# A selective scan in a two-layer block: the product with C on GpSimd, the scan's input in PSUM, channels in two halves

## The chip, the core and the metric

The kernel runs on one core of one Trainium2 chip. The core has five engines that work from queues of their own: TensorE (PE; PEld is its loading of weights), VectorE (DVE), ScalarE (ACT), GpSimd (POOL) and SyncE (SP), which here only starts DMAs. SBUF and PSUM are its on-chip memories of 128 partitions; matmuls write to PSUM, in 8 banks of 512 float32 columns. The metric is device microseconds of one execution, the median of several runs.

## The reference, cut to what matters

Two layers, each with adaptive normalisation, over 2048 tokens of width 512. The first is a block-masked linear layer and a gated feed-forward layer with low-rank additions. The second is a selective state-space layer (1024 channels, 16 states each) and a linear layer with a top-2 choice of low-rank experts. The change touches the second layer's scan, and the normalisations of both:

```python
def _layernorm(x, axis=-1, eps=1e-05):
    m = jnp.mean(x, axis=axis, keepdims=True)
    v = jnp.var(x, axis=axis, keepdims=True)
    return (x - m) / jnp.sqrt(v + eps)
...
dt = jax.nn.softplus(ts @ W_dt.T + b_dt)
A = -jnp.exp(A_log.astype(jnp.float32))

def step(state, inp):
    dt_t, B_t, C_t, u_t = inp
    dA = jnp.exp(dt_t[..., None] * A)
    state = state * dA + (dt_t * u_t)[..., None] * B_t[:, None, :]
    y = jnp.einsum('bdn,bn->bd', state, C_t)
    return (state, y)
...
y = ys.transpose(1, 0, 2) + x * D
y = y * jax.nn.silu(gate)
return y @ W_out.T
```

## The kernel before, in words

All is float32. The 2048 tokens are cut into 8 chunks of 256 (`TC`); a chunk's activations are two tiles of 128 tokens (`NM`) by 512. The 1024 channels of the scan are 8 tiles (`ND`) of 128 channels, one channel to a partition, with time along the columns.

For a chunk c and each of the 16 states n the loop at the end of the kernel does this:

- `decays` (L455): eight ScalarE exponentials, one per channel tile, write exp(dt * A) into `da` (two buffers, taken in turn).
- L669, VectorE: dt*u times row n of B, which is broadcast to all partitions, goes into `hb` (two buffers).
- L671, VectorE: one scan over 8 x 258 = 2064 columns, in place in `hb`. Each channel tile has two columns more than its 256 (`SEG = TC + 2`): one with zero decay that clears the state, and one that holds the state carried from the chunk before. `S.copy` at L681 puts it there from `states`, and L673 saves the new one.
- L677, VectorE: `hb` times row n of C goes into `hc` (two buffers).
- `add_t` (L438), TensorE: 16 transposes add `hc` to the accumulators `ys`, four PSUM banks with tokens on the partitions. They are issued one state later, behind the next scan (`due`).

`rows_bc` (L460) loads row n of B and C for a chunk by a broadcast DMA of 256 KB on SyncE's queue, three states ahead; four buffers. Behind the first state of a chunk, `gating` (L483) multiplies the finished `ys` of the chunk before by the gate, and `skip` (L446) begins the new sums with u*D. `steps` (L419: dt by a matmul and a softplus) and `inputs` (L429: dt*u) prepare the next chunk at its predecessor's last state.

The matmul work of the other layers is written as generators. The loop takes pieces of them at every state by a budget in microseconds of TensorE work: `first` runs the first layer of later chunks (`first_layer`, L265), `second` (`beside`, L622) the output projection (`out_proj`) of the chunk before, the gate projection (`gate_proj`), the front part of the next chunk (`front`: norm, input projection, convolution at L391) and the experts of the chunk before. Weights come from memory again for each chunk, in 256 KB loads on SyncE's queue, through 12 `ws` buffers. Within each engine's queue the instructions keep one fixed order, which the planner of the language chose.

`norm_t` (L144), four times per chunk, takes mean and variance on VectorE (L148, L149), the inverse root on GpSimd (L151, L152), applies both on VectorE (L156), and transposes on TensorE. In `front`, GpSimd also copies the convolution's three halo columns in and out (L379, L382). L256 is a GpSimd product of 128x512 in the preparation of weights, before the loop. PSUM is full: four banks for matmuls (`ps_mm`), four for `ys`.

Of the kernel before, what the change touches and what calls it, by code (L numbers as in the profile page):

```python
# [17 lines left out]
P = 128  # L18
# [5 lines left out]
R = 16  # L24
DI, NS, RDT, KC = 1024, 16, 32, 4
ND = DI // P
SEG = TC + 2
E = 8
EA = E * R
LN_EPS, RMS_EPS = 1e-5, 1e-6  # L30
# [7 lines left out]
def mamba_block_kernel(  # L38
# [17 lines left out]
    tpool = ctx.enter_context(tc.tile_pool(name="tmp", bufs=5))  # L56
    hpool = ctx.enter_context(tc.tile_pool(name="hT", bufs=1))
    hid = ctx.enter_context(tc.tile_pool(name="hid", bufs=6))
    upool = ctx.enter_context(tc.tile_pool(name="u", bufs=ND // 2))
    zpool = ctx.enter_context(tc.tile_pool(name="z", bufs=2 * NM))  # L60
    bcp = ctx.enter_context(tc.tile_pool(name="bc", bufs=4))
    dram = ctx.enter_context(tc.tile_pool(name="dram", bufs=1, space=DRAM))
    ps_mm = ctx.enter_context(tc.tile_pool(name="ps_mm", bufs=4, space=PSUM))
    ps_y = ctx.enter_context(tc.tile_pool(name="ps_y", bufs=1, space=PSUM))

    def tmp():
        return tpool.tile([P, DM], FP, tag="t", name="tmp")
# [7 lines left out]
    def halves(t):  # L75
        return t.rearrange("p (a n) -> p a n", a=2)
# [18 lines left out]
            nc.sync.dma_start(out=xt, in_=x_in[i * P : (i + 1) * P, :])  # L95
            xs[c].append(xt)

    da = [keep.tile([P, ND, SEG], FP, name=f"da{i}") for i in range(2)]
    hb = [keep.tile([P, ND, SEG], FP, name=f"hb{i}") for i in range(2)]
    hc = [keep.tile([P, ND, TC], FP, name=f"hc{i}") for i in range(2)]  # L100
    dtu = keep.tile([P, ND, TC], FP, name="dtu")
    dt = keep.tile([P, ND, TC], FP, name="dt")
    states = keep.tile([P, NS, ND], FP, name="states")

    def mod_weights(wmod, j, queue):
        wms = []
# [37 lines left out]
    def norm_t(xt, scale, shift, tag):  # L144
        st = small.tile([P, NM, 6], FP, tag="st", name="st")
        mv = small.tile([P, NM, 2], FP, tag="mv", name="mv")
        for m in range(NM):
            V.bn_stats(st[:, m, :], xt[m])  # L148
            V.bn_aggr(mv[:, m, :], st[:, m, :])  # L149
        rs = small.tile([P, NM], FP, tag="rs", name="rs")  # L150
        G.tensor_scalar(rs, mv[:, :, 1], LN_EPS, None, ALU.add)  # L151
        G.tensor_tensor(rs, rs, power, ALU.pow)  # L152
        xn = []
        for m in range(NM):
            t = tmp()
            V.tensor_scalar(t, xt[m], mv[:, m, 0:1], rs[:, m : m + 1], ALU.subtract, ALU.mult)  # L156
            xn.append(t)
        h = hpool.tile([P, NK, TC], FP, tag=tag, bufs=2 if tag == "h0" else 1, name="h")
        for k2 in range(NK // 2):
            ps = halves(bank())  # L160
            for i in range(2):
                k = 2 * k2 + i
                for m in range(NM):
                    T.transpose(ps[:, i, m * P : (m + 1) * P], xn[m][:, k * P : (k + 1) * P], ident)  # L164
            for i in range(2):
                k = 2 * k2 + i
                S.activation(  # L167
                    h[:, k, :], ps[:, i, :], AF.Identity, bias=shift[:, k : k + 1], scale=scale[:, k : k + 1]
                )
            yield 0.5  # L170
        return h
# [43 lines left out]
    sb, cb = (mod_col("a", c0_sb, wmod0, j, nc.scalar) for j in (3, 4))  # L215
    gb = mod_gate(scb0, wmod0, 5, nc.scalar)

    ranks = [hc[0].rearrange("p t n -> p (t n)")[:R, i * DM : (i + 1) * DM] for i in range(3)]
    wides = [t.rearrange("p t n -> p (t n)")[:R, :FF] for t in (da[0], da[1], hb[0])]
    for dst, src in zip(ranks + wides, (gate_a, up_a, down_bt, gate_bt, up_bt, down_a)):  # L220
        nc.gpsimd.dma_start(out=dst, in_=src)
    ga_r, ua_r, db_r = ranks
# [121 lines left out]
    S.activation(neg_a, ch[:, :, C_A : C_A + NS], AF.Exp)  # L344
    V.tensor_scalar(neg_a, neg_a, -1.0, None, ALU.mult)
    for t in da:
        G.memset(t[:, :, 0:2], 0.0)
    for t in hb:
        G.memset(t[:, :, 0:2], 0.0)
    G.memset(states, 0.0)  # L350

    halo = None
    fed = {}
# [62 lines left out]
        fed[c] = (h, us, ssm, bc)  # L416
        yield 0.5

    def steps(c):  # L419
        us, ssm = fed[c][1:3]  # L420
        for t in range(ND):
            ps = bank()
            T.matmul(
                ps[:, :TC], lhsT=wdt[:, t * P : (t + 1) * P], rhs=ssm[:RDT, :], start=True, stop=True
            )
            dst, src, b_dt = dt[:, t, :], ps[:, :TC], ch[:, t, C_DT : C_DT + 1]
            S.activation(dst, src, AF.Softplus, bias=b_dt)

    def inputs(c):  # L429
        us = fed[c][1]  # L430
        for t2 in range(ND // 2):
            V.tensor_tensor(
                dtu[:, 2 * t2 : 2 * t2 + 2, :], dt[:, 2 * t2 : 2 * t2 + 2, :], us[t2], ALU.mult
            )

    ys = [[ps_y.tile([P, DM], FP, name=f"y{m}{a}") for a in range(2)] for m in range(NM)]

    def add_t(t, src, first, last):  # L438
        for m in range(NM):
            a, i = t // 4, t % 4  # L440
            T.matmul(  # L441
                ys[m][a][:, i * P : (i + 1) * P], lhsT=src[:, m * P : (m + 1) * P], rhs=ident,
                start=first and i == 0, stop=last, is_transpose=True, skip_group_check=True,
            )

    def skip(c):  # L446
        us = fed[c][1]
        for t2 in range(ND // 2):
            ud = halves(tmp())
            for i in range(2):  # L450
                t = 2 * t2 + i
                S.activation(ud[:, i, :], us[t2][:, i, :], AF.Identity, scale=ch[:, t, C_D : C_D + 1])
                add_t(t, ud[:, i, :], True, False)

    def decays(n):  # L455
        d = da[n % 2]
        for t in range(ND):
            S.activation(d[:, t, 2:], dt[:, t, :], AF.Exp, scale=neg_a[:, t, n : n + 1])  # L458

    def rows_bc(c, n):  # L460
        bcn = bcp.tile([P, 2, TC], FP, tag="bcn", name="bcn")
        nc.sync.dma_start(out=bcn, in_=fed[c][3][:, n, :].partition_broadcast(P))
        return bcn

    zs = {}

# [13 lines left out]
            for m in range(NM):  # L480
                S.activation(zs[c][2 * m + a], acc[m], AF.Silu)  # L481

    def gating(c):  # L483
        for m in range(NM):
            for a in range(2):
                z = zs[c][2 * m + a]
                V.tensor_tensor(z, z, ys[m][a], ALU.mult)

    def out_proj(c):
        xt = xs[c]  # L490
# [131 lines left out]
    def beside(c):  # L622
# [9 lines left out]
        if c > 0:  # L632
            yield from experts(c - 1)

    for _ in front(0):
        pass
    steps(0)
    inputs(0)
    bcs = [rows_bc(0, n) for n in range(3)]
    decays(0)  # L640
    first = ahead()
    ended = False

# [7 lines left out]

    due = None
    left = 0.0
    for c in range(NC):
        second = beside(c)
        spare, finished = 0.0, False
        for n in range(NS):
            h, d, hcn, bcn = hb[n % 2], da[n % 2], hc[n % 2], bcs.pop(0)
            if n + 1 < NS:
                decays(n + 1)  # L660
            if n == NS - 3:
                while not finished:
                    cost = next(second, "end")
                    finished = cost == "end"
                    if cost is None:
                        run_first(0.1)
            if n == NS - 1 and c + 1 < NC:
                steps(c + 1)
            V.tensor_tensor(h[:, :, 2:], dtu, bcn[:, 0:1, :].to_broadcast([P, ND, TC]), ALU.mult)  # L669
            flat_h, flat_d = h.rearrange("p t n -> p (t n)"), d.rearrange("p t n -> p (t n)")  # L670
            V.tensor_tensor_scan(flat_h, flat_d, flat_h, 0.0, ALU.mult, ALU.add)  # L671
            if c + 1 < NC:
                S.copy(states[:, n, :], h[:, :, SEG - 1])  # L673
            if due is not None:
                for t in range(ND):
                    add_t(t, due[:, t, :], False, n == 0)
            V.tensor_tensor(hcn, h[:, :, 2:], bcn[:, 1:2, :].to_broadcast([P, ND, TC]), ALU.mult)  # L677
            due = hcn
            if n + 1 < NS or c + 1 < NC:
                if c + (n + 1) // NS > 0:  # L680
                    S.copy(hb[(n + 1) % 2][:, :, 1], states[:, (n + 1) % NS, :])  # L681
            if n == 0:
                if c > 0:
                    gating(c - 1)
                skip(c)
            if n + 3 < NS:
                bcs.append(rows_bc(c, n + 3))
            elif c + 1 < NC:
                bcs.append(rows_bc(c + 1, n + 3 - NS))
            if n == NS - 1 and c + 1 < NC:  # L690
                inputs(c + 1)
                decays(0)
            budget = 4.8 if c > 0 or n > 7 else 2.5
            spare += budget
            while spare > 0 and not finished:
                cost = next(second, "end")
                finished = cost == "end"
                if cost is None or finished:
                    break
                spare -= cost  # L700
            left = run_first(left + (3.6 if c > 0 or n > 7 else 8.0) + (0.0 if finished else max(spare, 0.0)))
            spare = min(spare, 0.0)
    for t in range(ND):
        add_t(t, due[:, t, :], False, True)
    gating(NC - 1)
    for gen in (first, out_proj(NC - 1), experts(NC - 1)):
        for _ in gen:
            pass
# [73 lines left out]
```

## Time and profile before

| | us |
|---|---|
| median of 3 runs (lowest to highest) | 1860.17 (1859.12 to 1862.04) |
| the profiled execution | 1859.38 |
| its span, first to last instruction | 1857.6 |
| first scan (L671) starts | 246.9 |
| last product with C (L677) ends | 1808.7 |
| first scan of a chunk to the first of the next, chunks 0 to 6 | 221, 206, 209, 198, 198, 201, 184 |

Spans and starts are counted from the first instruction. A row of the table of groups names line, engine, operation, output from inputs, shapes and count; behind the bar stand the busy time and the mean duration in ns, behind the next one the idle time of the engine just before the group, and what ended it. L numbers are lines of the kernel before, and of the changed kernel where the text says so. In the waits, a line says which engine and line waited for which, how long in total, how often, and the longest. In the timeline, a line is a piece of one engine's work: start, length, line, operation.

### The profile page before, as it was taken

How to read it: one execution, taken by the hardware profiler on the slowest of the kernel's cores; microseconds unless marked ns; L12 is line 12 of the kernel's file. 1: busy time of each engine (PE TensorE's matmuls, PEld its weight loads, DVE VectorE, ACT ScalarE, POOL GpSimd, SP SyncE). 2: the span in 40 equal slices, each digit the busy share in tenths (PEclk: the TensorE clock that was granted, in tenths of full speed). 3: DMA queues.
4: the chain of work that ended last, by engine and by line, in shares of the span. 5: the costliest groups of instructions: out<-in, count | busy, mean ns of one | idle time of the engine just before them, and what ended most of it. 6: DMA issues, size and time to landing. Idle time of an engine off the chain costs nothing. (4 is left out here: it accounts for less than half of the span.)

```text
span 1857.6 us, 18733 instructions
## 1 busy us (share of the span) xinstructions
PE 1562.9 (84%) x6568; PEld 1079.8 (58%) x6568; DVE 1483.0 (80%) x1215; ACT 938.9 (51%) x2005; POOL 225.7 (12%) x211
## 2 busy tenths in 40 slices
PE   4899879988698888999799888999899789768646
PEld 4685647756465665576456665576557565544433
DVE  2222387797978989897999789897989799999992
ACT  0110367445654565565565566466556555674521
POOL 0123010013000200031003300160003000300000
PEclk9689779988998989999899999999999999879768
DMA  8544333562343234432343334422333235213100
GB/s 251 154 154 165 116 86 115 166 198 85 91 126 108 86 93 120 129 102 89 91 137 106 94 100 123 116 83 89 116 115 100 80 104 149 67 35 100 28 20 12
DMA packets 157536, 199.73 MB, mean 108 GB/s; under 512 B 14962, under 2 KB 93682, under 8 KB 157443
## 3 DMA queue, kind: packets, MB, share of 16 engines
q1 hardware_dynamic: 141984, 166.57, 31.0%
q10 hardware_dynamic: 10434, 15.81, 2.6%
q0 software_dynamic: 5024, 16.16, 2.4%
q8 instruction: 52, 0.85, 0.2%
q14 instruction: 42, 0.34, 0.1%
HBM read 182.43 MB, written 16.06 MB: 107 GB/s over the span
## 5 line engine op out<-in xcount | busy, mean ns | idle before, releaser
L671 DVE TENSOR_TENSOR_SCAN hb<-da,hb 128x2064 f32<-128x2064 f32 x128 | 568.7, 4449 | 3.5
L458 ACT ACTIVATE da<-dt,neg_a 128x256 f32<-128x256 f32 x1024 | 430.4, 497 | 55.9 <-DVE hb L671 43.1
L298 PE MATMUL ps<-h,ws 128*128 128x256 f32 (+1 forms) x1408 | 352.6, 407 | 19.6 <-ACT z L481 13.0
L441 PE MATMUL y<-ident,hc 128*128 128x128 f32 x2048 | 287.0, 293 | 65.5 <-DVE hc L677 65.3
L298 PEld LDWEIGHTS ps<-h,ws 128*128 128x128 f32 (+1 forms) x1408 | 281.6, 204 | 93.2 <-issue 19.6
L441 PEld LDWEIGHTS y<-ident,hc 128*128 128x128 f32 x2048 | 255.1, 152 | 117.8 <-DVE hc L677 75.4
L677 DVE TENSOR_TENSOR hc<-hb,bcn 128x2048 f32<-128x2048 f32 x128 | 291.4, 2278 | 35.8 <-PE y L441 35.6
L669 DVE TENSOR_TENSOR hb<-dtu,bcn 128x2048 f32<-128x2048 f32 x128 | 290.7, 2281 | 2.7
L673 ACT COPY states<-hb 128x8 f32<-128x8 f32 x112 | 22.8, 203 | 348.0 <-DVE hb L671 340.1
L151 POOL TENSOR_SCALAR rs<-mv 128x2 f32<-128x2 f32 x32 | 41.3, 1292 | 1155.4 <-DVE mv L149 1139.5
L508 PE MATMUL ps<-ws,tmp 128*128 128x512 f32 x256 | 136.3, 671 | 47.3 <-ACT tmp L502 47.1
L317 PE MATMUL ps<-ws,hidden 128*128 128x512 f32 (+1 forms) x352 | 159.0, 601 | 5.7 <-ACT z L481 4.9
L371 PE MATMUL ps<-h,ws 128*128 128x256 f32 x512 | 122.2, 394 | 2.5 <-ACT h L167 2.5
L476 PE MATMUL ps<-ws,h 128*128 128x512 f32 x256 | 117.1, 604 | 1.1 <-ACT hidden L306 0.6
L317 PEld LDWEIGHTS ps<-ws,hidden 128*128 128x128 f32 (+1 forms) x352 | 65.7, 192 | 85.1 <-issue 71.7
L371 PEld LDWEIGHTS ps<-h,ws 128*128 128x128 f32 x512 | 100.3, 199 | 21.3 <-ACT h L167 5.8
L508 PEld LDWEIGHTS ps<-ws,tmp 128*128 128x128 f32 x256 | 51.2, 214 | 101.3 <-ACT tmp L502 53.5
L309 DVE TENSOR_TENSOR hidden<-hidden,tmp 128x512 f32<-128x512 f32 x40 | 27.6, 690 | 85.1 <-ACT tmp L307 85.1
L391 DVE SCALAR_TENSOR_TENSOR tmp<-xp,ch,tmp 128x256 f32<-128x256 f32 x192 | 79.7, 476 | 13.1 <-ACT tmp L386 12.6
L458 ACT ACT_TABLE_LOAD x67 | 86.0, 1283 | 1.0
L164 PE MATMUL ps<-ident,tmp 128*128 128x128 f32 x256 | 48.7, 329 | 41.4 <-DVE tmp L156 38.0
L379 POOL COPY xp<-halo 128x6 f32<-128x6 f32 x28 | 71.0, 2537 | 77.2 <-DVE tmp L391 66.7
(137 smaller groups left out, 1575.0 us busy)
## 6 DMA issues: line engine op xcount, KB each, us to landing
bcn<-bc SPq DMA_DIRECT2D x128, 256.0 KB, 5.1
ws<-gate_s SPq DMA_DIRECT2D x70, 256.0 KB, 2.7
ws<-up_s SPq DMA_DIRECT2D x70, 256.0 KB, 2.7
ws<-down_s SPq DMA_DIRECT2D x70, 256.0 KB, 3.8
ws<-win_x_t_dram SPq DMA_DIRECT2D x64, 256.0 KB, 3.8
ws<-win_z_t_dram SPq DMA_DIRECT2D x64, 256.0 KB, 2.9
ws<-wout_s SPq DMA_DIRECT2D x64, 256.0 KB, 2.6
ws<-wmod_dram ACTq DMA_DIRECT2D x36, 256.0 KB, 3.2
```

The costliest lines, as they stand in the source:

```text
L298: T.matmul(ps[:n, i, :], lhsT=w3[:, k, :], rhs=h[:, k, :], stop=k == NK - 1, **start_only(4 * i + k),)
L317: T.matmul(acc[m], lhsT=hidden[j // 2][:n, j % 2, m * P : (m + 1) * P], rhs=w[:n, :], start=j == 0, stop=j == len(HT) - 1,)
L371: T.matmul(ps[:, i, :], lhsT=w3[:, k, :], rhs=h[:, k, :], stop=k == NK - 1, **start_only(4 * i + k),)
L379: G.tensor_copy(xp[:, :, : KC - 1], halo[:, 2 * t2 : 2 * t2 + 2, :])
L391: V.scalar_tensor_tensor(acc[:, i, :], xp[:, i, j : j + TC], ch[:, t, C_W + j : C_W + j + 1], acc[:, i, :], ALU.mult, ALU.add,)
L441: T.matmul(ys[m][a][:, i * P : (i + 1) * P], lhsT=src[:, m * P : (m + 1) * P], rhs=ident, start=first and i == 0, stop=last, is_transpose= ...
L458: S.activation(d[:, t, 2:], dt[:, t, :], AF.Exp, scale=neg_a[:, t, n : n + 1])
L476: T.matmul(acc[m], lhsT=h[:, k, m * P : (m + 1) * P], rhs=w, start=k == 0, stop=k == NK - 1)
L508: T.matmul(acc[m], lhsT=g[:, i, m * P : (m + 1) * P], rhs=w, start=t == 0, stop=t == ND - 1)
L669: V.tensor_tensor(h[:, :, 2:], dtu, bcn[:, 0:1, :].to_broadcast([P, ND, TC]), ALU.mult)
L671: V.tensor_tensor_scan(flat_h, flat_d, flat_h, 0.0, ALU.mult, ALU.add)
L677: V.tensor_tensor(hcn, h[:, :, 2:], bcn[:, 1:2, :].to_broadcast([P, ND, TC]), ALU.mult)
```

## The change

- The channels are scanned in two halves of four tiles (`NA = 2`, `TH = 4`): a chunk is now 32 half-steps q = (c, a, n) of 1024 columns, all states of half 0 first. `da`, `hb` and `hc` have three buffers of half the width; dt, dt*u and the states one per half.
- The padding columns are gone. Column 0 of each tile has zero decay, and the carried state, multiplied by that step's decay (`carry`), is added to the first column of dt*u*B by a small VectorE operation.
- dt*u*B goes to `bx`, two PSUM banks (new pool `ps_b`); `ys` shrinks to two banks, for one half. The scan reads `da` from SBUF and `bx` from PSUM, and writes `hb`.
- The product with C moves from VectorE to GpSimd, as two instructions of 128x512 per half-step.
- Gating and skip run once per half, at n = 1, in front of that step's `add_t`. `steps` and `inputs` run per half, at n = 12 (`NS - 4`) of the half before. The next chunk's front has to be through at n = 10 of half 1; before, it was n = 13.
- The broadcast rows of B and C are loaded for each half-step, four ahead, into six buffers; decays run two half-steps ahead. The budgets per half-step are half of those per state. `u` has six buffers.
- `norm_t` applies mean and inverse root on ScalarE, as scale and bias; VectorE makes the bias (`off`).

```diff
@@ norm_t
+        off = small.tile([P, NM], FP, tag="off", name="off")
+        V.scalar_tensor_tensor(off, mv[:, :, 0], -1.0, rs, ALU.mult, ALU.mult)
...
-            V.tensor_scalar(t, xt[m], mv[:, m, 0:1], rs[:, m : m + 1], ALU.subtract, ALU.mult)
+            S.activation(t, xt[m], AF.Identity, bias=off[:, m : m + 1], scale=rs[:, m : m + 1])
@@ inputs(c, a)
+        if c > 0:
+            first = dt[a][:, :, 0:1].to_broadcast([P, TH, NS])
+            V.tensor_tensor(carry[a], neg_a[:, a * TH : (a + 1) * TH, :], first, ALU.mult)
+            S.activation(carry[a], carry[a], AF.Exp)
+            V.tensor_tensor(carry[a], carry[a], states[a], ALU.mult)
@@ decays(q)
-            S.activation(d[:, t, 2:], dt[:, t, :], AF.Exp, scale=neg_a[:, t, n : n + 1])
+            S.activation(da[q % 3][:, i, 1:], dt[a][:, i, 1:], AF.Exp, scale=neg_a[:, t, n : n + 1])
@@ the loop
+    AHEAD = 4
...
+    for q, (c, a, n) in enumerate(ALL):
...
+        h, d, hcn, bcn = hb[q % 3], da[q % 3], hc[q % 3], bcs.pop(0)
+        if q + AHEAD < len(ALL):
+            bcs.append(rows_bc(ALL[q + AHEAD][0], ALL[q + AHEAD][2]))
...
+        nxt = (c, 1) if a == 0 else (c + 1, 0)
+        if n == NS - 4 and nxt[0] < NC:
+            steps(*nxt)
+            inputs(*nxt)
+        if q + 2 < len(ALL):
+            decays(q + 2)
-            V.tensor_tensor(h[:, :, 2:], dtu, bcn[:, 0:1, :].to_broadcast([P, ND, TC]), ALU.mult)
-            flat_h, flat_d = h.rearrange("p t n -> p (t n)"), d.rearrange("p t n -> p (t n)")
-            V.tensor_tensor_scan(flat_h, flat_d, flat_h, 0.0, ALU.mult, ALU.add)
+        V.tensor_tensor(bx, dtu[a], bcn[:, 0:1, :].to_broadcast([P, TH, TC]), ALU.mult)
+        if c > 0:
+            V.tensor_tensor(bx[:, :, 0], bx[:, :, 0], carry[a][:, :, n], ALU.add)
+        V.tensor_tensor_scan(
+            h.rearrange("p t n -> p (t n)"), d.rearrange("p t n -> p (t n)"),
+            bx.rearrange("p t n -> p (t n)"), 0.0, ALU.mult, ALU.add,
+        )
...
-            V.tensor_tensor(hcn, h[:, :, 2:], bcn[:, 1:2, :].to_broadcast([P, ND, TC]), ALU.mult)
+        for i in range(0, TH, 2):
+            G.tensor_tensor(
+                hcn[:, i : i + 2, :], h[:, i : i + 2, :], bcn[:, 1:2, :].to_broadcast([P, 2, TC]), ALU.mult
+            )
+        if n == 1:
+            if q > NS:
+                gating(*ALL[q - 2][:2])
+            skip(c, a)
+        if due is not None:
+            for i in range(TH):
+                add_t(i, due[:, i, :], False, n == 0)
+        due = hcn
+        spare += 2.4 if c > 0 or a == 1 else 1.25
```

## The prediction

> **What bounds the kernel now.** I read the busy times first. They name two candidates, TensorE and VectorE, and an almost idle GpSimd.
>
> ```profile
> PE 1562.9 (84%) x6568; PEld 1079.8 (58%) x6568; DVE 1483.0 (80%) x1215; ACT 938.9 (51%) x2005; POOL 225.7 (12%) x211
> ```
>
> An average over stages does not tell them apart, so I cut the span at the first scan of each chunk (starts of L671: 247, 468, 675, 883, 1081, 1280, 1480 and 1664 us) and asked for the busy times per stretch. Columns: stretch, length, busy us of PE, PEld, DVE, ACT, POOL, granted clock, DMA share, GB/s. The last line shown runs from the last chunk's first scan to the last product.
>
> ```profile
> 883.00:1081.00 198.00, 173.46 (x752) 117.52 (x752) 178.02 (x140) 118.34 (x257) 29.72 (x18) 0.94 0.37 107
> 1081.00:1280.00 199.00, 177.80 (x750) 121.83 (x751) 179.50 (x142) 116.03 (x250) 36.52 (x18) 0.93 0.36 105
> 1280.00:1480.00 200.00, 175.99 (x760) 119.29 (x758) 176.91 (x136) 121.12 (x261) 16.59 (x16) 0.92 0.33 102
> ...
> 1664.00:1808.00 144.00, 92.03 (x374) 62.96 (x374) 142.14 (x78) 64.81 (x158) 4.03 (x4) 0.73 0.18 48
> ```
>
> VectorE works 178.1 of 199 us in a middle chunk (89.5%) and 142.1 of 144 in the last one. PE's 176 overstate it, since its matmuls are pipelined. The chain of waits, whose columns are start, length, work, shows what a matmul costs when packed:
>
> ```profile
> 1544.32 3.69 PE ps L298 x16
> 1548.01 1.75 PE y L441 x16
> ...
> 1560.09 8.59 PE ps L317 x20
> ```
>
> That is 0.231 us for 256 columns, 0.109 for a transpose of 128, 0.429 for 512. With the counts of the table of groups: 1120 of 512 columns (L317, L476, L508, L280, L600), 2176 of 256 (L298, L371, L402, L423), 2688 of 128 (L441 with 128 from the skip path, L164, L497, L550): 480 + 503 + 293 = 1276 us, 159 per chunk, and 163 with L272 and L610 (64 of 512 columns). So TensorE needs 163 of 199 us (82%), and VectorE leads. The waits agree: ScalarE's longest are for the scan.
>
> ```profile
> ACT states L673 <- DVE hb L671: 340.1, 96, 8.9
> ```
>
> What VectorE spends is three rows, 2281 + 4449 + 2278 = 9.0 us per state n, 144 of its 178 us per chunk:
>
> ```profile
> L671 DVE TENSOR_TENSOR_SCAN hb<-da,hb 128x2064 f32<-128x2064 f32 x128 | 568.7, 4449 | 3.5
> L677 DVE TENSOR_TENSOR hc<-hb,bcn 128x2048 f32<-128x2048 f32 x128 | 291.4, 2278 | 35.8 <-PE y L441 35.6
> L669 DVE TENSOR_TENSOR hb<-dtu,bcn 128x2048 f32<-128x2048 f32 x128 | 290.7, 2281 | 2.7
> ```
>
> **The shared port.** GpSimd's timeline shows small operations stretched by VectorE: a copy of 128x6 takes 0.19 us beside L285 (one SBUF and one PSUM input), and 6.53 us when L677 and two L669, which read two SBUF tiles, run until 1032.05.
>
> ```profile
> 1006.35 0.19 POOL L379 COPY xp<-halo 128x6 f32<-128x6 f32 x1 [3.12 <-DVE tmp L391]
> 1025.58 6.53 POOL L379 COPY xp<-halo 128x6 f32<-128x6 f32 x1 [1.53 <-DVE tmp L391]
> 1006.11 0.68 DVE L285 TENSOR_TENSOR x<-x,ps 128x512 f32<-128x512 f32 x1
> 138.32 1.05 DVE L309 TENSOR_TENSOR hidden<-hidden,tmp 128x512 f32<-128x512 f32 x1 [8.72 <-ACT tmp L307]
> ```
>
> The last line is the other direction: L309 (mean 0.69) took 1.05 when it met L256, a GpSimd product already running. So a VectorE operation with two SBUF inputs and a reading GpSimd operation exclude each other; one with a single SBUF input is free.
>
> **The change, part by part.** A half-step q replaces half of a state n.
>
> Product with dt*u*B (L669 to PSUM): 512 and 2048 columns took 688 (L432) and 2281 ns, a line of 0.157 + 1.037 per 1000 columns: 1.22 us for 1024. No row writes PSUM; reading it costs nothing extra (L245 685, L323 675, L432 with two SBUF tiles 688). Bounds per operation: -0.01 from these rows, +0.35 if it met what L309 met; I take 0. Scan over 1024: (4.449 - 0.157)/2064 per column gives 2.29 us, 0 for the PSUM input by the same rows. [...] The add of the carried state, 128x4: 0.17 us, like the small rows (L570 168 ns), chunks 1 to 7. Three operations that depend on each other: L671 started 0.10 us behind the end of L669, while independent ones overlap by 0.08. So 1.22 + 0.10 + 0.17 + 0.10 + 2.29 - 0.08 = 3.80 us per q, 121.6 per chunk against 144 now.
>
> The padding columns, 16 per state, are in that line (0.03 us per n). The norm's application leaves VectorE: 4 x 537 ns (L156, two per norm, four norms: 8 x 0.537 = 4.3 us per chunk) against 4 x 0.17 for the new offset. Carry products add about 0.9. VectorE per chunk: 178.1 - 144 + 121.6 - 4.3 + 0.7 + 0.9 = 153 us.
>
> ScalarE takes 8 x 0.60 us (L306's length) per chunk, loses 14 copies into the scan's input (L681, 195 ns), gains 14 state copies (L673, 203) and, since softplus now comes twice per chunk, about 2 table loads of 1.28: 118 to about 126 us. It is not the bound, but the norm waits there for VectorE's offset, and the decays stand behind it.
>
> GpSimd's product: L256, 128x512, ran unheld in 1.257 to 1.285 us, so 2.53 per q and 81 per chunk. Bounds: 1.26, and 1.72, its longest (held). When a scan ends, VectorE's next product is already queued and takes the port for 1.22; GpSimd follows with 2.53 and is through 3.75 us after the scan, VectorE's next scan at 3.80. They just fit; a miss costs VectorE at most 1.27, and I take 5 us per chunk.
>
> [...]
>
> Also on GpSimd's queue: the norm's L151 and L152 (0.22 + 0.72) and the halo copies L379 and L382, 16 operations per chunk, now stand behind products. VectorE waits for the first (offset) and the third (convolution), 8 places per chunk. Now these cost 14.0 us in the whole span (L156 waiting for L152). Bounds per place: 0, and 6.53, the held copy above; I take 1.2, near the 0.9 that such a place costs now where it costs anything (14.0 us, 16 times): 10 us per chunk.
>
> The queue of SyncE gets 128 more broadcasts of 256 KB (33.5 MB on 199.7; DMA share 0.36 to about 0.43). Each now waits for the GpSimd product two steps back, with the weight loads behind it; four are asked for ahead, some 15 us against 5.1 to land: I price it at 0, and where that cover fails TensorE waits for weights. PSUM: the y accumulators shrink to one half, so the hand-over (transposes, gating, transposes) comes 16 times, not 8. It cost 20.9 + 6.7 us for 8; 3 us more per chunk, hidden on an engine with slack if VectorE leads no longer.
>
> **Sum.** VectorE: 153 + 5 + 10 = 168 us; TensorE 163. Both lie far below 199, but now level. VectorE as sole leader fills 89.5% today; two engines that wait for each other fill less, and I take 86%: 163/0.86 = 190, against 202 for the mean of chunks 1 to 5 (206, 209, 198, 198, 201), so 12.5 x 5 = 63. Chunk 0 (221 us, two first layers) 12 and chunk 6 (184) 12. The last chunk is VectorE alone: 32 x 3.80 + 2.53 + 5 = 129 against 142, 13. Before the first scan, half the softplus, decays and dt*u: 3. The tail, 51 us, stays. Together 103 off a span of 1857.6; with 1.8 around it the profiled run took 1859.4, 0.8 below the median. Forecast 1757.
>
> **Rivals.** (a) More: the engines keep 89.5% and the GpSimd places cost nothing: 163/0.895 = 182, 20 x 5 + 2 x 18 + 16 = 152 off, 1708. ScalarE's waits for the scan get shorter, which speaks for it. It lies in the forecast's own range, 1690 to 1815.
> (b) The gain turns into waits: TensorE and VectorE in lockstep at 196, 6 us off each of seven chunks or none: 1860 - 42 - 16 = 1802 or 1844; I give it 1815 to 1855. For it: buffers now hold 3 half-steps (11 us) instead of 2 steps (18), and a burst like L317's 8.59 us fills that.
> (c) Slower: GpSimd's in-order queue becomes a serial link. The offset and the halo copies wait behind products, VectorE stands still, and the products start late. At the upper price, 8 places x 6.53 = 52 us: (153 + 52)/0.895 = 229 us per chunk, 27 x 7 = 189 more, less 16 at both ends: 2032; at 4.5 us per place 211 and 1907. It decides from 26 us per chunk (153 + 26 = 179), 3.3 per place. Against it: the same small operations are held 2 to 4 us today, and VectorE hardly waits.
> (d) It does not do what it says: scan and GpSimd exclude each other even with one input in PSUM. Then 153 + 81 = 234 us per chunk, 261 at 89.5%: 59 x 7 = 413 more, and 32 x 2.53 = 81 in the last chunk less its 18 of the scans: about 2330. L285 speaks against it.
>
> [...]
>
> **How the numbers follow.** Forecast with (a) 0.55, (b) 0.18, (c) 0.18, (d) 0.05, no change 0.04. A difference within 0.2% can't be told from none here. Faster 0.73, same 0.04, slower 0.23. The range leaves out (d), the worst of (c) and what lies under 1680: 1680 to 1890.
>
> **What would show it.** Right: the new scan at 2.29 us on a PSUM input, L256's length in the product, 1.22 for dt*u*B, middle chunks near 190 us with VectorE near 85% and GpSimd near 50%. Wrong: GpSimd products well over 1.3 us while scans run (d), VectorE idle before the offset, the convolution or a scan with GpSimd as releaser (c), or the same period with both engines under 85% (b).

## The result and the profile after

The changed kernel is slower: 1908.26 us (1904.61 to 1914.97), against 1861.11 for the kernel before on the same chip, a ratio of 1.0259 (95% interval 1.0226 to 1.0292). The profiled execution took 1914.97, its span is 1913.2 us. Two of the runs further down, rings_of_four and rows_and_rings, had one execution of over 8300 us each; their times here are medians of their other three. In this part L numbers are lines of the kernel that the line shown belongs to.

The busy times of the changed kernel:

```profile
PE 1577.2 (82%) x6568; PEld 1075.1 (56%) x6568; DVE 1385.8 (72%) x1563; ACT 1003.0 (52%) x2093; POOL 879.3 (46%) x721
```

VectorE has 97 us less work than before (1483.0), where the forecast counted about 200, and works 72% of the span instead of 80%. No engine leads. Two chunks in the cut by first scans, columns as before, against 198 and 199 us for the same two before:

```profile
892.60:1101.00 208.40, 176.81 (x762) 120.76 (x761) 170.96 (x189) 128.51 (x271) 103.16 (x82) 0.91 0.45 120
1101.00:1315.20 214.20, 178.78 (x762) 119.72 (x761) 168.03 (x189) 127.59 (x268) 101.70 (x82) 0.91 0.43 117
```

The groups of the parts that changed, from the table of groups:

```profile
L697 POOL TENSOR_TENSOR hc<-hb,bcn 128x512 f32<-128x512 f32 x512 | 777.1, 1538 | 642.1 <-PE y L450 469.7
L690 DVE TENSOR_TENSOR_SCAN hb<-da,bx 128x1024 f32<-128x1024 f32 x256 | 584.7, 2284 | 117.4 <-POOL hc L697 91.9
...
L687 DVE TENSOR_TENSOR bx<-dtu,bcn 128x1024 f32<-128x1024 f32 x256 | 356.2, 1392 | 11.3 <-DMA bcn<-bc 5.0
...
L394 DVE SCALAR_TENSOR_TENSOR tmp<-xp,ch,tmp 128x256 f32<-128x256 f32 x192 | 115.5, 649 | 19.9 <-ACT tmp L389 19.1
...
L315 DVE TENSOR_TENSOR hidden<-hidden,tmp 128x512 f32<-128x512 f32 x40 | 38.9, 971 | 81.1 <-ACT tmp L313 81.1
```

The same convolution and gated product in the kernel before:

```profile
L309 DVE TENSOR_TENSOR hidden<-hidden,tmp 128x512 f32<-128x512 f32 x40 | 27.6, 690 | 85.1 <-ACT tmp L307 85.1
L391 DVE SCALAR_TENSOR_TENSOR tmp<-xp,ch,tmp 128x256 f32<-128x256 f32 x192 | 79.7, 476 | 13.1 <-ACT tmp L386 12.6
```

The scan has the length that was forecast, 2.284 us. The operations with two SBUF inputs have not: the convolution (L394) took 476 ns before and 649 now, the gated product (L315) 690 and 971, dt*u*B 1392 instead of the forecast 1220. GpSimd's product took 1538 instead of the forecast 1265, and GpSimd stood idle for 470 us until transposes had freed an `hc` buffer; the scan stood 92 us for GpSimd, which still held `hb`.

The timeline of VectorE and GpSimd shows how they meet. First a free stretch of the last chunk:

```profile
1731.11 1.23 DVE L687 TENSOR_TENSOR bx<-dtu,bcn 128x1024 f32<-128x1024 f32 x1
...
1732.68 2.29 DVE L690 TENSOR_TENSOR_SCAN hb<-da,bx 128x1024 f32<-128x1024 f32 x1
1735.00 1.23 DVE L687 TENSOR_TENSOR bx<-dtu,bcn 128x1024 f32<-128x1024 f32 x1
...
1731.21 3.48 POOL L697 TENSOR_TENSOR hc<-hb,bcn 128x512 f32<-128x512 f32 x2 [0.41 <-issue]
1735.10 2.25 POOL L697 TENSOR_TENSOR hc<-hb,bcn 128x512 f32<-128x512 f32 x1 [0.41 <-issue]
```

Here the two fit: a half-step takes 3.89 us, GpSimd is held until dt*u*B ends and is through at 1734.69, 0.3 us before the next one. Some ninety microseconds later they do not:

```profile
1825.09 7.03 DVE L687 TENSOR_TENSOR bx<-dtu,bcn 128x1024 f32<-128x1024 f32 x1
...
1822.39 0.63 POOL L625 DMA_DIRECT2D out_dram<-x  x1 [8.53 <-DVE bx L689]
1823.05 3.72 POOL L697 TENSOR_TENSOR hc<-hb,bcn 128x512 f32<-128x512 f32 x3
1826.71 0.58 POOL L625 DMA_DIRECT2D out_dram<-x  x1
1827.31 3.71 POOL L697 TENSOR_TENSOR hc<-hb,bcn 128x512 f32<-128x512 f32 x3
```

GpSimd had fallen behind: it had stood 8.53 us before a store (L625) of the experts' result, which VectorE writes until 1822.09 (L623), with products behind it in its queue, and then ran six of them one after the other. The dt*u*B that arrived at 1825.09 ended at 1832.12, 1.10 us after the last of them (1831.02), not between two. This long collision happens once in the execution. Of the 256 dt*u*B, 58 last more than 1.3 us, and all of these but this one at most 2.32. All 256 together are stretched by 41 us.

### The profile page after: what moved, and what is told of

It is laid out like the page before. It is cut to its first block, busy times and chain, and to the rows that moved or that the text cites. A ratio compares the mean times of both kernels' runs of the same rounds, so it can differ in the third digit from the quotient of the medians.

```text
span 1913.2 us, 20659 instructions
## 1 busy us (share of the span) xinstructions
PE 1577.2 (82%) x6568; PEld 1075.1 (56%) x6568; DVE 1385.8 (72%) x1563; ACT 1003.0 (52%) x2093; POOL 879.3 (46%) x721
## 5 line engine op out<-in xcount | busy, mean ns | idle before, releaser
L697 POOL TENSOR_TENSOR hc<-hb,bcn 128x512 f32<-128x512 f32 x512 | 777.1, 1538 | 642.1 <-PE y L450 469.7
L690 DVE TENSOR_TENSOR_SCAN hb<-da,bx 128x1024 f32<-128x1024 f32 x256 | 584.7, 2284 | 117.4 <-POOL hc L697 91.9
L469 ACT ACTIVATE da<-dt,neg_a 128x255 f32<-128x255 f32 x1024 | 440.9, 497 | 65.3 <-DVE hb L690 48.7
L687 DVE TENSOR_TENSOR bx<-dtu,bcn 128x1024 f32<-128x1024 f32 x256 | 356.2, 1392 | 11.3 <-DMA bcn<-bc 5.0
L450 PE MATMUL y<-ident,hc 128*128 128x128 f32 x2048 | 303.2, 293 | 49.7 <-POOL hc L697 49.0
L695 ACT COPY states<-hb 128x4 f32<-128x4 f32 x224 | 43.5, 196 | 367.5 <-DVE hb L690 353.8
L520 PE MATMUL ps<-ws,tmp 128*128 128x512 f32 x256 | 151.8, 739 | 63.4 <-ACT tmp L514 63.3
L394 DVE SCALAR_TENSOR_TENSOR tmp<-xp,ch,tmp 128x256 f32<-128x256 f32 x192 | 115.5, 649 | 19.9 <-ACT tmp L389 19.1
L315 DVE TENSOR_TENSOR hidden<-hidden,tmp 128x512 f32<-128x512 f32 x40 | 38.9, 971 | 81.1 <-ACT tmp L313 81.1
L162 ACT ACTIVATE tmp<-x,off,rs 128x512 f32<-128x512 f32 x64 | 48.9, 806 | 87.8 <-DVE mv L153 46.0
L170 PEld LDWEIGHTS ps<-ident,tmp 128*128 128x128 f32 x256 | 39.5, 178 | 72.6 <-ACT tmp L162 60.9
```

The source lines that it names most:

```text
L394: V.scalar_tensor_tensor(acc[:, i, :], xp[:, i, j : j + TC], ch[:, t, C_W + j : C_W + j + 1], acc[:, i, :], ALU.mult, ALU.add,)
L450: T.matmul(ys[m][:, i * P : (i + 1) * P], lhsT=src[:, m * P : (m + 1) * P], rhs=ident, start=first and i == 0, stop=last, is_transpose=Tru ...
L469: S.activation(da[q % 3][:, i, 1:], dt[a][:, i, 1:], AF.Exp, scale=neg_a[:, t, n : n + 1])
L520: T.matmul(acc[m], lhsT=g[:, i, m * P : (m + 1) * P], rhs=w, start=t == 0, stop=t == ND - 1)
L687: V.tensor_tensor(bx, dtu[a], bcn[:, 0:1, :].to_broadcast([P, TH, TC]), ALU.mult)
L690: V.tensor_tensor_scan(h.rearrange("p t n -> p (t n)"), d.rearrange("p t n -> p (t n)"), bx.rearrange("p t n -> p (t n)"), 0.0, ALU.mult, ...
```

## The experiments

Each time is a median of several runs; ratios are to the kernel before on the same chips (1854.9 to 1859.4 us in these, 1861.1 for the changed kernel, so that differences of a few us between runs mean nothing), and the changed kernel's own is 1.0259. Five theories were tried: L, the port on which the prediction has VectorE and GpSimd exclude each other (its name for what holds them; the traces show the lengths alone): GpSimd's reads stretch VectorE's two-input operations; T, the short buffers and the length of the chain through GpSimd; Q, GpSimd's in-order queue; H and N, the hand-over between halves and the norm on ScalarE.

**small_product: the same instructions and waits, hardly any product.**

```diff
-                hcn[:, i : i + 2, :], h[:, i : i + 2, :], bcn[:, 1:2, :].to_broadcast([P, 2, TC]), ALU.mult
+                hcn[:, i : i + 2, 0:8], h[:, i : i + 2, 0:8], bcn[:, 1:2, 0:8].to_broadcast([P, 2, 8]), ALU.mult
```

> The changed kernel, but GpSimd's product with C covers only 8 of every 256 columns (the rest of the product is left out). All instructions and waits stay, the product's length and its hold on the shared port go. Theory L (the port: VectorE's operations with two SBUF inputs are stretched by 147 us in all): 1908 - 130 to 150 = about 1770. Theory T (VectorE is tied to TensorE through three short buffers, since GpSimd waits 470 us for the transposes that free hc): the tie stays, so only some 40 to 60 us go, 1850 to 1870. Theory H (hand-over of the halves): under 30 us, 1880 or more.

Measured 1745.84, ratio 0.9398 (0.9377 to 0.9420): 162 us less than the changed kernel, although GpSimd still waits for the transposes (729 us). The product itself, by its length or its reads, costs it all.

**fill_no_read: GpSimd's busy time back, without most of the reads.**

```diff
+            for _ in range(2):
+                G.memset(hcn[:, i : i + 2, :], 0.0)
```

> Like the run with the small product (8 of every 256 columns, the rest left out), but in front of each small product GpSimd clears the same 128x512 twice, so that it is busy again without reading SBUF. Theory L (VectorE is stretched because GpSimd reads SBUF): the stretch stays away and the time stays near the small product's, 1746 to 1790. Theory T (the length of the product in the chain from scan to transposes, through short buffers, whatever it reads): the time comes back in proportion to GpSimd's length, 1850 to 1910 if a cleared pair takes as long as a product.

Measured 1762.34, 0.9510 (0.9467 to 0.9552). The groups on GpSimd and the same three on VectorE:

```profile
L698 POOL MEMSET hc<- 128x512 f32 x1024 | 497.8, 524 | 462.3 <-PE y L450 460.6
L699 POOL TENSOR_TENSOR hc<-hb,bcn 128x16 f32<-128x16 f32 x512 | 206.8, 418 | 161.1 <-DVE hb L690 78.3 <-issue 47.8 <-DVE top L580 11.1
...
L687 DVE TENSOR_TENSOR bx<-dtu,bcn 128x1024 f32<-128x1024 f32 x256 | 315.4, 1232 | 11.6 <-DMA bcn<-bc 5.0
L394 DVE SCALAR_TENSOR_TENSOR tmp<-xp,ch,tmp 128x256 f32<-128x256 f32 x192 | 80.5, 479 | 18.1 <-ACT tmp L389 17.5
...
L315 DVE TENSOR_TENSOR hidden<-hidden,tmp 128x512 f32<-128x512 f32 x40 | 28.0, 699 | 73.6 <-ACT tmp L313 73.5
```

Two clears and a small product last 2 x 524 + 418 = 1466 ns where the product lasted 1538, and GpSimd is nearly as busy as in the changed kernel (784 against 879 us). VectorE's operations are back at their lengths, and VectorE's busy time falls by 127 us against the changed kernel:

```profile
PE 1531.8 (87%) x6568; PEld 1040.6 (59%) x6568; DVE 1258.6 (72%) x1563; ACT 1026.4 (58%) x2109; POOL 784.4 (45%) x1745
```

Group by group, dt*u*B gives back 41 of these 127 us, the convolution 35, dt*u 14, the gated product 12, the products for the carry 9, the new offset 8 (its 128x2 took 415 ns on average instead of 158), and other small ones the rest.

Of the 162 us, 16 come back with GpSimd's busy time, and 146 do not. But the run does not restore one part of the length, the way from a scan to its finished `hc`: the clears do not wait for the scan. From a half-step of the last chunk:

```profile
1701.62 2.85 POOL L698 MEMSET hc<- 128x512 f32 x6
1701.76 2.29 DVE L690 TENSOR_TENSOR_SCAN hb<-da,bx 128x1024 f32<-128x1024 f32 x1
...
1704.08 1.23 DVE L687 TENSOR_TENSOR bx<-dtu,bcn 128x1024 f32<-128x1024 f32 x1
...
1704.44 1.13 POOL L699 TENSOR_TENSOR hc<-hb,bcn 128x16 f32<-128x16 f32 x2
```

Where nothing else is late, `hc` is ready 1.52 us behind the scan here and in small_product, and 3.61 us behind it in the changed kernel. Of the 2.1 us between, 1.0 is GpSimd's wait for dt*u*B and 1.1 the product's length (one_sbuf_input, below, has 2.63). So the 146 us belong to the reads and to this 1.1 us per half-step together; no run separates them.

**one_sbuf_input: the product in full, one SBUF input less in dt*u*B.**

```diff
-        V.tensor_tensor(bx, dtu[a], bcn[:, 0:1, :].to_broadcast([P, TH, TC]), ALU.mult)
+        V.tensor_tensor(bx, dtu[a], bx, ALU.min)
```

> The changed kernel, with GpSimd's product in full; VectorE's dt*u*B has the same length, but takes the minimum of dt*u (SBUF) and the old contents of bx (PSUM), so it reads SBUF once (B is left out of the computation). Theory L (the port): its 43 us of stretch go, and GpSimd need not wait for it, 1.22 us per half-step; the stretch of the convolution, the gated product and dt*u (some 65 us) stays: 1830 to 1870. Theory T (length of the chain through GpSimd): only the shorter wait of GpSimd counts, 1880 to 1908. If the port is nothing: 1908.

Measured 1838.36, 0.9888 (0.9874 to 0.9903), 70 us less than the changed kernel, with 61 us less work on VectorE (1324.9). From the groups:

```profile
L688 DVE TENSOR_TENSOR bx<-dtu,bx 128x1024 f32<-128x1024 f32 x256 | 313.8, 1226 | 6.0
L394 DVE SCALAR_TENSOR_TENSOR tmp<-xp,ch,tmp 128x256 f32<-128x256 f32 x192 | 107.8, 611 | 20.3 <-ACT tmp L389 19.5
```

dt*u*B is unstretched, the convolution is not. GpSimd no longer waits for dt*u*B either: its product takes 1304 ns instead of 1538, and `hc` is ready 2.63 us behind a free scan. The two directions of this one meeting are worth 70 of the 146 us. The other 76 go with GpSimd's reads or with the shorter way to `hc` in fill_no_read; the convolution, dt*u, the gated product, the carry and the offset are what the reads still stretch here.

**scan_input_in_sbuf and before_product_on_gpsimd: the scan reads SBUF twice.** In the first, dt*u*B goes to `h` instead of `bx`; the second is the kernel before with four GpSimd products of 128x512 per state in place of L677.

> The changed kernel with dt*u*B written to hb in SBUF, so that the scan reads SBUF twice, in place. Theory L: scan and product now exclude each other too; a half-step takes 1.22 + 0.17 + 2.29 + 2.53 + 0.2 = 6.4 us instead of 3.9: 205 us in the last chunk (142.6 now), and some 45 us more in each other chunk: 2250 to 2350. If a scan that reads SBUF twice leaves GpSimd alone: 1908.

> The kernel before with nothing but the product with C moved to GpSimd, as four instructions of 128x512 per state; dt*u*B stays in SBUF, the scan reads SBUF twice. Theory L: product, scan and dt*u*B take turns: 2.28 + 4.44 + 4 x 1.27 = 11.8 us per state instead of 9.0, 45 us more per chunk: 2150 to 2250. If GpSimd's work were free beside VectorE's: 1858 - 291 of VectorE's work, bounded by TensorE, 1750.

Measured 2164.98, 1.1642 (1.1625 to 1.1659), and 2114.82, 1.1372 (1.1353 to 1.1391); both less than L expected, and far above what its rivals did. In the first, the scan is stretched and dt*u*B waits for GpSimd to free `hb`:

```profile
L690 DVE TENSOR_TENSOR_SCAN hb<-da,hb 128x1024 f32<-128x1024 f32 x256 | 673.9, 2643 | 15.3 <-ACT da L469 4.8 <-DVE hb L689 0.9
L687 DVE TENSOR_TENSOR hb<-dtu,bcn 128x1024 f32<-128x1024 f32 x256 | 400.3, 1571 | 162.1 <-POOL hc L697 157.5 <-DMA bcn<-bc 4.4
```

The PSUM input is worth 257 us (2165 against 1908): that part of the change does what it says.

**product_on_vector and product_split: all or half of the product on VectorE.**

```diff
+        V.tensor_tensor(hcn[:, 0:2, :], h[:, 0:2, :], bcn[:, 1:2, :].to_broadcast([P, 2, TC]), ALU.mult)
+        G.tensor_tensor(hcn[:, 2:4, :], h[:, 2:4, :], bcn[:, 1:2, :].to_broadcast([P, 2, TC]), ALU.mult)
```

> The changed kernel with the product with C on VectorE, one instruction of 1024 columns per half-step (1.22 us); halves, PSUM input and ScalarE's norm stay. GpSimd's coupling (port and waits) is gone, and VectorE has 256 x 1.22 = 312 us more and 147 us of stretching less: 1386 - 147 + 312 = 1551 us of work against 1483 in the kernel before. If GpSimd alone is what costs (L or T), VectorE leads again with the fill it had before: 1858 + (1551 - 1483)/0.9 = about 1930. If the halves themselves cost (H), more: 1960 to 2000.

> The changed kernel with the product of two channel tiles on VectorE (128x512, 0.69 us) and of the other two on GpSimd. VectorE has 256 x 0.69 = 177 us more to do; GpSimd reads half as long. Theory L with a stretch in proportion to GpSimd's reading: 147 / 2 less on VectorE, so 100 us more in all, most of it in VectorE's idle time: 1880 to 1910. If GpSimd's one instruction fits beside the scan whole, so that nothing is stretched: 1840 to 1870.

All on VectorE: 1894.47, 1.0198 (1.0173 to 1.0223), less than the 1930 expected and less than the changed kernel. Taking 312 us of work off VectorE bought nothing: here it works 145 us more than in the changed kernel (1530.9), and the time is 14 us less. Split: 1966.82, 1.0576 (1.0550 to 1.0601), outside both expectations. Half the reads, but one more two-input operation to meet; VectorE and GpSimd in its timeline:

```profile
1885.75 0.69 DVE L696 TENSOR_TENSOR hc<-hb,bcn 128x512 f32<-128x512 f32 x1
1886.36 2.31 DVE L687 TENSOR_TENSOR bx<-dtu,bcn 128x1024 f32<-128x1024 f32 x1
...
1885.78 1.79 POOL L697 TENSOR_TENSOR hc<-hb,bcn 128x512 f32<-128x512 f32 x1 [3.85 <-DVE hb L690]
```

GpSimd's product, issued beside VectorE's half, takes 1.79 us, and the dt*u*B behind that half 2.31 where a free one takes 1.23: a full collision, also where nothing else is late. Of the 256 dt*u*B, 84 last more than 1.3 us, 24 of them in the last chunk.

**rings_of_four, lean_gpsimd, steps_early, norm_on_vector: the waits.** Four `hb` and four `hc` buffers; halo copies on ScalarE and stores on SyncE's queue; `if n == (3 if a == 0 else NS - 4)` for the next half's steps; the norm's old line.

> The changed kernel with four hb and four hc buffers of half a state instead of three and three, in one tile. Theory T (short buffers): the scan's wait for GpSimd (92 us) and GpSimd's wait for the transposes shrink by a third or more: 30 to 60 us less, 1850 to 1880. Theory L: within 10 us of 1908.

> The changed kernel with GpSimd's halo copies moved to ScalarE and its output stores to SyncE's queue; the norm's two small operations stay. Theory Q (the in-order GpSimd queue: a store that waits for the experts' result, or a halo copy that waits for the convolution, holds the products behind it; GpSimd lost 46 + 62 + 22 us before them): 30 to 60 us less, 1850 to 1880. Theories L and T: within 15 us of 1908.

> The changed kernel with the second half's softplus and dt*u issued at n = 3 of the first half instead of n = 12. Theory H (dt comes late at the hand-over; VectorE's dt*u waits 54 us for ScalarE): some 30 to 40 us less, 1870 to 1880. Theories L and T: within 10 us of 1908.

> The changed kernel with the norm applied by VectorE again, as before. Theory N (the norm on ScalarE's in-order queue waits for the offset and holds the decays behind it, 42 us): 20 to 30 us less, about 1880. Theories L and T: VectorE gets 64 x 0.54 us more work, most of it in idle time, 0 to 15 us more, 1908 to 1925.

Measured: 1884.57, 1.0153 (1.0111 to 1.0196); 1912.43, 1.0313 (1.0284 to 1.0341); 1917.88, 1.0326 (1.0300 to 1.0352); 1932.10, 1.0406 (1.0383 to 1.0428). Q, H and N fall: neither an emptier GpSimd queue nor an earlier dt gains, and the norm on ScalarE is a gain of 24 us here. T keeps 24 us, between the two readings. Even these need not be the wait alone: with deeper buffers VectorE's busy time falls from 1385.8 to 1355.1.

**before_norm_on_scalar: that part alone.**

> The kernel before with nothing but the norm applied by ScalarE. VectorE leads there at 89.5%, and loses 64 x 0.54 - 32 x 0.17 = 29 us of work: 29/0.9 = 32 us less, about 1828, if ScalarE's in-order queue takes it without a new wait. If its wait for the offset holds the decays: 1850 to 1875.

Measured 1851.22, 0.9993 (0.9971 to 1.0015): nothing. VectorE has 25 us less work (1458.1), and waits more, for example for the offset:

```profile
DVE off L154 <- POOL rs L152: 24.5, 25, 1.3
```

**three_banks, three_banks_rows, rows_and_rings: a kernel that computes everything and reads SBUF once in dt*u*B.** Row n of B has to lie in PSUM, which was full.

```diff
-    ps_mm = ctx.enter_context(tc.tile_pool(name="ps_mm", bufs=4, space=PSUM))
+    ps_mm = ctx.enter_context(tc.tile_pool(name="ps_mm", bufs=3, space=PSUM))
...
+        S.copy(brow[(q + 1) % 2], bcs[0][:, 0, :])
-        V.tensor_tensor(bx, dtu[a], bcn[:, 0:1, :].to_broadcast([P, TH, TC]), ALU.mult)
+        V.tensor_tensor(bx, dtu[a], brow[q % 2].unsqueeze(1).to_broadcast([P, TH, TC]), ALU.mult)
```

> The changed kernel, rebuilt so that three PSUM banks do for matmuls: the output projection takes one tile of tokens after the other (its weights are loaded twice, 128 x 256 KB more in all), the experts transpose before they take their banks. All is computed. A control: fewer banks and more loads cost TensorE 0 to 60 us, 1905 to 1970.

> As three_banks, and the freed bank holds row n of B on all partitions, copied there by ScalarE (256 copies of 128x256, some 0.37 us each, 95 us on an engine that is about 53% busy). dt*u*B then reads SBUF once, and all is computed. Theory L: 60 to 75 us less than three_banks, as one_sbuf_input was 70 less than the changed kernel. Theory T: within 15 us of three_banks, or more for ScalarE's copies.

> As three_banks_rows with four hb and four hc buffers, as in rings_of_four. If what is left comes from products that start late, when a transposition frees their buffer, and so meet VectorE's other operations: another 15 to 30 us less, as rings_of_four took 21 off the changed kernel. If the rows in PSUM have removed those meetings already: within 10 us of three_banks_rows.

Measured 1986.87, 1.0686 (1.0668 to 1.0703); 1930.50, 1.0382 (1.0365 to 1.0399); 1921.17, 1.0338 (1.0318 to 1.0358). The rebuilding costs 79 us, more than expected; the rows take 56 of them back, a little under L's 60 to 75, and new waits for ScalarE's copies show what the rest went to:

```profile
L683 DVE TENSOR_TENSOR bx<-dtu,brow 128x1024 f32<-128x1024 f32 x256 | 314.1, 1227 | 83.3 <-ACT brow L685 62.7 <-ACT brow L682 5.8 <-ACT states L693 0.5
```

The deeper buffers add 9 us, within the 10 of the second reading. VectorE works 48 us less in three_banks_rows than in three_banks (1321.4 against 1369.3). No run that computes everything beats the kernel before.

## Why the prediction was wrong

It forecast 1757 us, 5.5% less, and the time rose by 2.6%. The step that failed is the price of the meetings with GpSimd's products: "They just fit; a miss costs VectorE at most 1.27, and I take 5 us per chunk." For dt*u*B alone that was the right size, 41 us in all, 5 per chunk. But it stood for all of them. Measured, VectorE's operations are longer by 127 us (1385.8 against 1258.6 with most of the reads taken away), 16 per chunk, and the kernel by 146. Three things were wrong:

- The list. Every other VectorE operation with two SBUF inputs stood at nothing, without a reason: the convolution, dt*u, the gated product, the carry, the offset, the small ones. Together they have 86 of the 127 us, 11 per chunk.
- The phase. The sum let GpSimd start right behind each dt*u*B. That holds where nothing else runs (3.89 us per half-step). Elsewhere GpSimd often starts late, when a transposition frees `hc` (132 such waits), at any moment of VectorE's work, and meets whatever runs there.
- The passing on. In the sum the stretch enters VectorE's 168 us alone, and the chunk is TensorE's 163/0.86 = 190: a longer VectorE operation costs nothing until VectorE leads. Measured, VectorE's work in chunks 1 to 5 is 168 us, the very number of the sum (16 of stretch where it had 5 and 10 of waits), and a chunk takes 211. By the estimate of 163 us TensorE fills 77% of it, not 86; in fill_no_read 85%.

So the stretch is not hidden. VectorE was only 72% busy in the changed kernel and in fill_no_read, and yet in the runs that keep the whole product 61 and 48 us less of VectorE work came with 70 and 56 us less of time (one_sbuf_input; three_banks_rows against three_banks). At that rate, some 1.15, the 127 us are worth about 147, an estimate, which leaves little of the 146 for the way to `hc`. A likely reason, read from the waits and not tested: VectorE's results release ScalarE's and TensorE's next work, and its idle time lies in other places. It is not VectorE's work as such that costs: in product_on_vector it works 145 us more in less time.

The bound of 1.27 us per miss held for 57 of the 58 long dt*u*B, and failed once, with the 7.03 us above. That one came of GpSimd's queue: in lean_gpsimd, where the stores are on SyncE's queue, no dt*u*B lasts more than 2.33 us, and the time is no better. That an operation "with a single SBUF input is free" holds for the scan, of which none of the 256 takes more than 2.289 us, but not for every operation: the norm, in the last part, is stretched, 858 ns against 537.

The rest of the sum stands. The single lengths were right: scan 2.284 against 2.29, carried state 0.167 against 0.17, product 1.27 at the median against 1.26 to 1.29, half-step 3.89 against 3.80. With the reads taken away (that run leaves most of the product out), the time is 1762 against the forecast of 1757, and chunks 1 to 5 take 192.5 us on average against 190; by the sum VectorE would have 200 us less work, by that run it has 224. So TensorE and VectorE block each other there about as assumed; VectorE's share of these chunks is 79%, not the 85% named. Terms that were smaller misses: the last chunk, 147.5 us from its first scan to its last product against 129 (134.4 in fill_no_read), with the long collision in it; dt*u's wait for ScalarE, 54 us, priced at nothing, which steps_early brings down (58 to 17 us in all) without a gain.

Of the rivals, (d) was rightly small: a scan with one PSUM input keeps its 2.28 us beside GpSimd's products. (c) had the right place, GpSimd, and the wrong mechanism: its in-order queue costs nothing that lean_gpsimd could show, and VectorE waits 19 us within the chunks for the norm's offset, and not at all for GpSimd before the convolution. Its third sign did come, a scan with GpSimd as releaser, 92 us; both together are 16 us per chunk, where it needed 26. (b) named half of the sign that came, both engines under 85% (VectorE 79, TensorE 77), but the short buffers it blamed are worth 24 us by rings_of_four. What decided was missing among the rivals: VectorE's other two-input operations beside GpSimd's product, 86 of the 127 us. The profile before had it: the line of L309 at 1.05 us was one such collision, and I priced it for dt*u*B alone.

Open: how the last 76 of the 146 us divide between these operations and the way to `hc`; and TensorE's granted clock, 0.881 in the changed kernel and 0.919 in fill_no_read. No run shows what sets it, or how much of the difference goes with it. It does not order the runs: one_sbuf_input has 0.867 in its profiled execution and 0.89 in the three others, with times within 1 us, and is 70 us faster than the changed kernel.

## What to carry to other kernels

Before work is moved from VectorE to GpSimd, list every VectorE operation in the same stretch that reads SBUF twice, not only the neighbours of the moved work: here the others had 86 of the 127 us of stretch, where GpSimd waited 132 times for TensorE's transposes and so started late. The price can be tested: let GpSimd write for the same length of time instead of reading (here 1466 ns where the product took 1538; VectorE's work fell by 127 us). See to it that these writes wait for what the moved work waited for; here they did not. Ask what the second engine leaves of a saving on the busiest one: VectorE was 89.5% busy in a middle chunk, and with the reads away 224 us less work on it were worth 93 us (1855.31 against 1762.34); 16 us of stretch per chunk took more than that back.

## What the runs showed of the hardware that was not expected

- Where GpSimd mostly writes SBUF, VectorE was next to unstretched: in fill_no_read, with GpSimd 45% busy, dt*u*B took 1232 ns and the convolution 479, against 1392 and 649 in the changed kernel, with GpSimd 46% busy.
- The dt*u*B of 7.03 us (7.06 in norm_on_vector, 4.61 in rings_of_four, at the same store) waited through several GpSimd products in a row: six of them ran from 1823.05 to 1831.02, with one store between, and it ended at 1832.12.
- A small operation was held about as long as a large one: in the changed kernel the offset's 128x2 took up to 1.22 us, 1.06 above its median of 0.16, and dt*u*B, but for the one of 7.03, up to 2.32, 1.09 above the 1.23 of a free one.
- A VectorE operation with one SBUF tensor was stretched as well: in norm_on_vector, beside GpSimd's products, the norm's 128x512 took 858 ns on average, against 537 in the kernel before.
- An input in PSUM cost the scan nothing: 2284 ns, where the same scan with two SBUF inputs has a median of 2286 in scan_input_in_sbuf (its mean, with the held ones, is 2643).
